# First half of batch 5 as seven block products, right sums of three batches placed anew

## The chip, the cores and the metric

The kernel runs on one core of a Trainium2 chip. The metric is the device time of one execution in microseconds (us); the time of a version is the median of its runs.

## What is computed

For each of 8 batches the input `x[b]` (1024 tokens, 512 features, float32) goes through two residual layers. Both are linear in `x` once the condition vector of the batch is known:

```python
# layer 0: a low-rank matrix per batch, from a small network on the condition
layer = base_layer[None] + einsum('bdr,bkr->bdk', x_a, x_b)      # rank 8
x = x + (x + einsum('btc,bco->bto', x, layer))
# layer 1: scaled weight
d = rsqrt(einsum('bi,io->bo', ys * ys, weight * weight) + 1e-8)  # ys = cond / sqrt(512)
x = x + (x + einsum('bsi,io->bso', x * ys[:, None, :], weight) * d[:, None, :])
```

So the output of a batch is `x[b]` times one 512 x 512 matrix of that batch, and the kernel builds these eight matrices (`q[b]`) first.

## The kernel before, in words

**Number format.** Float32 accuracy is made from two parts of each operand: a rounded high part and the rest (`h` and `l`, `ph` and `pl`, the two halves of `xs`). A product of two such operands takes three matmuls: high by high, high by rest, rest by high. ScalarE makes the high part by a cast, VectorE the rest by a subtraction that needs that cast.

**Plain tiles.** `main(b, t)` (L893) multiplies 128 tokens by `q[b]`: four chunks of 128 features, three matmuls each, so 12 matmuls of 512 columns into one bank `po`. ScalarE copies the bank to `o` and issues the store on its own queue. Tiles are numbered i = 8 b + t; `place(i)` names the spot behind tile i. The text calls "tile 36" the one with i = 36 (batch 4, t = 4). `split_x(b, j)` (L723) makes the operand `xs(b, j)` for two tiles, from a half batch `x(b, h)` that `load_x` (L719) brings in on SyncE's queue (1 MB).

**Seven products.** The last batches go by `Seven` (L905): a half batch g of 512 tokens is cut into 2 x 2 blocks, as `q[b]` is, and seven block products take the place of eight. A product is 12 matmuls of 256 columns. `make_sums` (L920) makes the right-hand sums of a batch: four subtractions `traw` of 512 columns on VectorE, two casts `th` of 1024 on ScalarE, two subtractions `tl` of 1024 on VectorE. `make_right` (L941) makes `ph` and `pl` of the batch. `make_left(g)` (L957) makes the left operands of a half: casts `xa`, `x22` and two `sh` on ScalarE; four sums `sraw`, then `xa`, `x22` and two `sl` on VectorE. It is a generator with six stops, and `part(g, steps)` (L1005) runs the seven products in the order 1, 5, 6, 2, 7, 3, 4, going one stop further in `steps` behind each. Products 1, 6, 7 and 4 add up in the same bank, `w`, which is emptied after each of them: by a ScalarE copy after 1, 6 and 4 and by a VectorE addition after 7. The next of them cannot start before that. Each part stores its 512 tokens on SyncE's queue.

**Buffers.** `x(b, h)`, `xs`, `xa`, the matrices `q[b]` and the `tl` tile of batch 5 share one pool, "big", of 8 buffers; `late_pools` (L1049) closes the pools of the earlier stages and opens those of the last.

**Order.** Matmuls keep the order of the program. The operations on VectorE, ScalarE and SyncE that go through `ve`, `se` and `sy` do so where `InOrder.on` is set, which is the case from behind the last tile on. While the tiles are emitted it is off (but for a few steps), and the planner of the programming layer puts each engine's instructions in the order of its list, by its own estimate of when they can run; it also decides which buffer of a pool a tile gets. On the chip each engine works its list from the top.

Before the change, batches 0 to 4 and the first half of batch 5 are plain tiles (0 to 43), and five parts follow: (5,1), (6,0), (6,1), (7,0), (7,1). The loop ends with:

```python
    InOrder.on = True
    load_x(NB - 2, 1)
    s5.part(1, s6.make_left(0))
```

Of the kernel before, what the change touches and what calls it, by code (L numbers as in the profile page):

```python
# [15 lines left out]
NB = 8  # L16
# [14 lines left out]
def cond_resid_kernel(ctx: ExitStack, tc: tile.TileContext, small, cond, condrows, consts,  # L31
# [47 lines left out]
    def big_tile(name, dtype=F32):  # L79
        return big.tile([P, KC, D], dtype, tag="big", name=name)  # L80
# [88 lines left out]
    def newton_rsqrt(v, sd, shape, name):  # L169

        r = sp.tile(shape, F32, name=f"r_{name}")
        ve.reciprocal(r, sd)
        t = sp.tile(shape, F32, name=f"t_{name}")
        ve.tensor_mul(t, r, r)
        ve.tensor_mul(t, t, v)
        ve.tensor_scalar(t, t, -0.5, 1.5, ALU.mult, ALU.add)
        return r, t
# [29 lines left out]
    r, t = newton_rsqrt(ve_l, sd, [NB, 1], "l")  # L207
# [86 lines left out]
    r, t = newton_rsqrt(v, sv, [P, KC, NB], "d")  # L294
# [163 lines left out]
    def rank_t():  # L458


        xb = with_bias(1)
        by = tmp_tile("by")
        ve.scalar_tensor_tensor(by, crow, SCALE, xb, ALU.mult, ALU.mult)
        hi, s = work_tile(), work_tile()
        se.copy(hi, by)
        yield
        ve.scalar_tensor_tensor(s, hi.bitcast(F32), neg_u, by, ALU.mult, ALU.add)
        by = s.bitcast(F32)
        yield
        pb = misc.tile([P, KC, P], F32, tag="misc", name="pb")  # L470
        for k in range(KC):
            turn(pb[:, k, :], by[:, k * P:(k + 1) * P], ident)
        byT = work_tile().rearrange("p (k c) -> p k c", k=KC)
        se.copy(byT, pb)
        yield
        pt = misc.tile([P, D], F32, tag="misc", name="pt_t")
        for k in range(KC):
            for i, w in enumerate((wh, wl)):
                mm(pt, byT[:, k, :], w[:, k, :], start=(k == 0 and i == 0),
                   stop=(k == KC - 1 and i == 1))  # L480
        t = tmp_tile("t")
        ve.tensor_mul(t, pt, drow)
        ve.scalar_tensor_tensor(t, xb, upper, t, ALU.mult, ALU.add)
        th, tl = work_tile(), work_tile()
        se.copy(th, t)
        yield
        ve.tensor_sub(tl, t, th.bitcast(F32))
        yield
        done = stack((th, tl), neg_t, "t", 0)
        yield  # L490
        stt[0] = done()
        yield
        late_rows.append(stack((th, tl), neg_t, "t", 1, rows[:, 3, :]))
        yield
# [208 lines left out]
    def p_tiles(b):  # L703
        ph[b] = ppool.tile([P, KC, D], F32R, tag="ph", name=f"ph_{b}")
        pl[b] = ppool.tile([P, KC, D], F32R, tag="pl", name=f"pl_{b}")
# [13 lines left out]
    def load_x(b, h):  # L719
        raw[b, h] = big_tile(f"x_{b}_{h}")  # L720
        sy.dma_start(raw[b, h], x[b, h])

    def split_x(b, j, part=None):  # L723

        t = raw[b, j // 2][:, :, (j % 2) * 2 * P:(j % 2 + 1) * 2 * P]
        if part != 1:
            xs[b, j] = big.tile([P, 2, KC, 2 * P], F32R, tag="big", name=f"xs_{b}_{j}")
            se.copy(xs[b, j][:, 0], t)
        if part != 0:
            hi, lo = xs[b, j][:, 0], xs[b, j][:, 1]  # L730
            ve.tensor_sub(lo, t, hi.bitcast(F32))
# [71 lines left out]
    steps = rank_t()  # L803
# [89 lines left out]
    def main(b, t):  # L893
        s = xs[b, t // 2]
        at = slice((t % 2) * P, (t % 2 + 1) * P)
        ps = po.tile([P, D], F32, tag="po", name=f"po_{b}_{t}")
        for c in range(KC):
            for i, (u, m) in enumerate(((0, ph[b]), (0, pl[b]), (1, ph[b]))):
                mm(ps, s[:, u, c, at], m[:, c, :],
                   start=(c == 0 and i == 0), stop=(c == KC - 1 and i == 2))  # L900
        o = pools["o"].tile([P, D], F32, tag="o", name=f"o_{b}_{t}")
        se.copy(o, ps)
        nc.scalar.dma_start(out[b, t * P:(t + 1) * P, :], o)
# [150 lines left out]
    NTT = NT // P  # L1054
    after = {}

    def at(b, t, f, *args):
        after.setdefault((b, t), []).append((f, args))
# [5 lines left out]
    place = lambda i: divmod(i, NTT)  # L1064
# [9 lines left out]
    for b, spots in ((4, [11 + n for n in spread]), (6, [21 + n for n in spread])):  # L1074
# [3 lines left out]
        for n, p in enumerate(Pair.ORDER):  # L1078
            spot = spots[2 * n]
# [5 lines left out]
        at(*place(first + 4), load_rank, b + 1)  # L1085
        at(*place(end), rank_term, b)
        at(*place(end + 1), rank_term, b + 1)
    for b, spot in ((4, 27), (5, 33)):
        for j in range(2):
            at(*place(spot + j), split_p, b, j)  # L1090

    s5, s6, s7 = (Seven(NB - i) for i in (3, 2, 1))

# [2 lines left out]
            pass  # L1096

    at(*place(31), late_pools)
    at(*place(34), s5.make_sums)
    at(*place(34), s5.share_right)  # L1100
    at(*place(35), s6.make_sums)
    at(*place(37), s7.make_sums)
    at(*place(38), load_x, NB - 3, 1)
    at(*place(39), all_left, s5, 1)
    at(*place(41), s6.make_right)
    at(*place(42), load_x, NB - 2, 0)

    TILES = (NB - 2) * NTT - NTT // 2
    for i in range(TILES):
        b, t = divmod(i, NTT)  # L1110
        if t == 0 and b + 1 < NB - 2:
            p_tiles(b + 1)
        main(b, t)
        if t % 4 == 0 and 0 < i < TILES - 4:
            load_x(*divmod(i // 4 + 1, NHALF))
        if t % 2 == 0 and i + 4 < TILES:
            split_x(*divmod(i // 2 + 2, NTT // 2))
        for f, args in after.get((b, t), ()):
            f(*args)
    InOrder.on = True  # L1120
    load_x(NB - 2, 1)
    s5.part(1, s6.make_left(0))
    load_x(NB - 1, 0)
    s6.part(0, s6.make_left(1))
    load_x(NB - 1, 1)
# [72 lines left out]
```

## Time and profile before

| what | us |
|---|---|
| median of 3 runs | 294.06 (293.91 to 294.32) |
| the profiled execution, its own time | 293.74 |
| its span, first to last instruction | 291.9 |
| TensorE busy | 286.3 (98%) |
| VectorE busy | 214.8 (74%) |
| ScalarE busy | 175.0 (60%) |
| mean granted clock of TensorE | 0.998 |

The page lists, for each engine, the busy time and its share of the span, then the chain of work that ended last, followed back from the end. In the timelines a row is: start, duration, engine, line, operation, what is written `<-` what is read, and in brackets the idle time before it with what ended it. PE is TensorE, PEld its weight loads, DVE VectorE, ACT ScalarE, SP SyncE. Durations of neighbouring rows can overlap by a tenth of a microsecond or more, since an engine starts the next instruction before the last one's result has landed.

### The profile page before, as it was taken

The page shows a single profiled execution, that of the slowest core. Times are in us where ns is not written, and L with a number is a line of the kernel's source. Part 1 is how long each engine was busy: PE and PEld are TensorE (multiplying, and loading weights), DVE is VectorE, ACT ScalarE, POOL GpSimd, SP SyncE. Part 2 cuts the span into 40 slices and gives each one's busy share as a digit, 9 for nine tenths or more (in the row PEclk, how much of TensorE's full clock was granted, in tenths as well). Part 3 has the DMA queues.
Part 4 walks back from the last instruction along what each step waited for, and adds up shares of the span by engine and source line. Part 5 has one row for each costly group of instructions (what it writes and reads, how often), then busy time and mean ns, then how long its engine had stood idle before and what let it go on. Part 6 is the DMA issues. An engine that isn't in the chain of part 4 may idle for free.

```text
span 291.9 us, 4100 instructions
## 1 busy us (share of the span) xinstructions
PE 286.3 (98%) x1519; PEld 225.2 (77%) x1519; DVE 214.8 (74%) x295; ACT 175.0 (60%) x272; POOL 35.9 (12%) x77
## 2 busy tenths in 40 slices
PE   7999999999999999999999999999999999999995
PEld 3665566467877878888877888887888889999994
DVE  2889898989916999519799565326789977798912
ACT  5757263286849884658654575544658745856641
POOL 2111000202944560000022000000000000000000
PEclk9999999999999999999999999999999999999999
DMA  7999999992799783332328114262175870852334
GB/s 209 405 429 413 411 403 405 390 383 90 187 321 322 235 250 116 110 145 93 159 80 263 55 72 135 83 216 74 72 251 176 291 257 1 290 204 87 142 146 144
DMA packets 19924, 62.14 MB, mean 213 GB/s; under 512 B 2736, under 2 KB 4016, under 8 KB 15552
## 3 DMA queue, kind: packets, MB, share of 16 engines
q1 hardware_dynamic: 9504, 43.76, 40.7%
q10 hardware_dynamic: 6912, 12.32, 11.5%
q0 software_dynamic: 3488, 5.79, 7.5%
q8 instruction: 12, 0.20, 0.3%
q14 instruction: 8, 0.07, 0.1%
HBM read 44.02 MB, written 17.84 MB: 212 GB/s over the span
## 4 chain that ended last, share of the span: by engine, by line
PE 96%; DMA 2%; ACT 0%; DVE 0%; SPq 0%; ACTq 0%; issue 0%
PE po L45 42%; PE pp L45 20%; PE sw L45 9%; PE px L45 5%; PE sz L45 5%; PE pg L45 4%; PE pq L45 4%; PE sv L45 2%; DMA b_raw<-in_baseT 2%; PE pr L45 1%; PE pt_t L45 1%; PE ps_t L45 0%; PE pq_v L45 0%; PE pq_z L45 0%; ACT o L62 0%; DVE o L62 0%
## 5 line engine op out<-in xcount | busy, mean ns | idle before, releaser
L45 PE MATMUL po<-ph,xs 128*128 128x512 f32 x352 | 113.7, 392 | 0.0
L45 PEld LDWEIGHTS po<-ph,xs 128*128 128x128 f32 x352 | 66.0, 188 | 15.6 <-issue 1.7
L45 PE MATMUL po<-pl,xs 128*128 128x512 f32 x176 | 68.6, 390 | 0.0
L62 ACT COPY o<-po 128x512 f32<-128x512 f32 x44 | 25.9, 588 | 35.0 <-PE po L45 35.0
L45 PEld LDWEIGHTS po<-pl,xs 128*128 128x128 f32 x176 | 33.0, 188 | 6.7
L62 DVE TENSOR_TENSOR xs<-x,xs 128x1024 fp32r<-128x1024 f32 (+1 forms) x23 | 27.0, 1176 | 15.0 <-ACT xs L62 15.0
L62 DVE TENSOR_TENSOR nl_p<-n,nh_p 128x1024 fp32r<-128x1024 f32 x21 | 25.7, 1222 | 12.4 <-ACT nh_p L62 12.4
L62 ACT CAST nh_p<-n 128x1024 fp32r<-128x1024 f32 x21 | 22.1, 1054 | 14.6 <-DVE n L62 10.9
L62 ACT CAST xs<-x 128x1024 fp32r<-128x1024 f32 x22 | 23.0, 1056 | 3.6 <-DMA x<-in_x 3.6
L62 ACT COPY q<-pp 128x512 f32<-128x512 f32 x30 | 17.4, 586 | 8.7 <-PE pp L45 8.6
L542 POOL DMA_DIRECT2D fa<-kept_a x28 | 13.8, 508 | 58.3 <-PE pr L45 54.0
L45 PE MATMUL pp<-nh_p,sh 128*128 128x512 f32 x48 | 19.0, 396 | 0.0
L45 PE MATMUL pp<-nh_p,sl 128*128 128x512 f32 x48 | 18.7, 390 | 0.0
L45 PE MATMUL pp<-nl_p,sh 128*128 128x512 f32 x48 | 18.7, 390 | 0.0
L62 DVE SCALAR_TENSOR_TENSOR n<-w_sb,ysT,d 128x512 f32<-128x512 f32 x24 | 16.9, 748 | 0.9 <-DMA d<-d_out 0.9
L62 ACT CAST sh<-sraw 128x1024 fp32r<-128x1024 f32 (+1 forms) x14 | 12.9, 926 | 6.8 <-DVE sraw L62 6.8
L62 DVE TENSOR_TENSOR sl<-sraw,sh 128x1024 fp32r<-128x1024 f32 (+1 forms) x14 | 14.9, 1067 | 2.2 <-ACT sh L62 2.2
L62 DVE TENSOR_TENSOR pl<-q,ph 128x1024 fp32r<-128x1024 f32 (+1 forms) x10 | 11.1, 1116 | 6.9 <-ACT ph L62 6.9
L45 PE MATMUL px<-w,hT 128*32 128x512 f32 x128 | 15.6, 599 | 0.0
L62 ACT COPY o<-sw 128x512 f32<-128x512 f32 (+1 forms) x12 | 6.2, 518 | 15.4 <-PE sw L45 12.3
L62 DVE TENSOR_TENSOR q<-pr,q 128x512 f32<-128x512 f32 x14 | 8.8, 688 | 7.9 <-PE pr L45 7.8
L62 DVE TENSOR_TENSOR n<-n,n 128x1024 f32<-128x1024 f32 x12 | 14.5, 1225 | 0.1
(199 smaller groups left out, 576.6 us busy)
## 6 DMA issues: line engine op xcount, KB each, us to landing
w<-in_w SPq DMA_DIRECT2D x16, 1024.0 KB, 10.4
x<-in_x SPq DMA_DIRECT2D x16, 1024.0 KB, 5.6
out<-o ACTq DMA_DIRECT2D x44, 256.0 KB, 2.3
out<-o SPq DMA_DIRECT2D x8, 512.0 KB, 2.9
fa<-kept_a POOLq DMA_DIRECT2D x28, 64.0 KB, 2.7
ft<-kept_t POOLq DMA_DIRECT2D x28, 64.0 KB, 3.5
d<-d_out POOLq DMA_DIRECT2D x6, 256.0 KB, 7.3
w_sb<-in_w SPq DMA_DIRECT2D x1, 1024.0 KB, 8.5
```

The lines of the kernel that those rows point to most:

```text
L45: tc.keep_in_program_order(nc.tensor.matmul(*args, **kw))
L62: return lambda *a, **kw: pin(f(*a, **kw)) if InOrder.on else f(*a, **kw)
L542: nc.gpsimd.dma_start(fold[name, b][32 * c:32 * c + 32, :], kept[name, g][32 * i:32 * i + 32, :])
```

## The change

The first half of batch 5 becomes a part (5,0) of seven products, ahead of (5,1), so that plain tiles end with tile 39. `split_p` and `split_x` for batch 5 fall away; `make_right` of batch 5 and `all_left` of (5,0) come in behind tiles 33 and 34. The right sums of batches 5, 6 and 7 stand behind tiles 31, 36 and 38, where they stood behind 34, 35 and 37. The left operands of (5,1), made at once behind tile 39 before, are now made step by step during part (5,0), one product later than in the other parts; `make_right` of batch 6 moves from behind tile 41 into part (5,1). All sums are VectorE subtractions and additions, as before.

```diff
-    for b, spot in ((4, 27), (5, 33)):
-        for j in range(2):
-            at(*place(spot + j), split_p, b, j)
+    for j in range(2):
+        at(*place(27 + j), split_p, 4, j)
...
     at(*place(31), late_pools)
-    at(*place(34), s5.make_sums)
-    at(*place(34), s5.share_right)
-    at(*place(35), s6.make_sums)
-    at(*place(37), s7.make_sums)
-    at(*place(38), load_x, NB - 3, 1)
-    at(*place(39), all_left, s5, 1)
-    at(*place(41), s6.make_right)
-    at(*place(42), load_x, NB - 2, 0)
-
-    TILES = (NB - 2) * NTT - NTT // 2
+    at(*place(31), s5.make_sums)
+    at(*place(32), load_x, NB - 3, 0)
+    at(*place(33), s5.make_right)
+    at(*place(34), all_left, s5, 0)
+    at(*place(36), load_x, NB - 3, 1)
+    at(*place(36), s6.make_sums)
+    at(*place(38), s7.make_sums)
+
+    def one_later(steps):
+        yield
+        yield from steps
+
+    TILES = (NB - 3) * NTT
     for i in range(TILES):
         b, t = divmod(i, NTT)
-        if t == 0 and b + 1 < NB - 2:
+        if t == 0 and b + 1 < NB - 3:
             p_tiles(b + 1)
         main(b, t)
...
     InOrder.on = True
+    load_x(NB - 2, 0)
+    s5.part(0, one_later(s5.make_left(1)))
     load_x(NB - 2, 1)
-    s5.part(1, s6.make_left(0))
+    s5.part(1, s6.make_left(0), then=s6.make_right)
     load_x(NB - 1, 0)
```

## The prediction

> **What bounds the kernel now.** I read the page's totals and chain first, then the table by stretches from 205 us on, then the timelines of TensorE (PE), ScalarE (ACT), VectorE (DVE) and SyncE (SP) around the places that the change touches, and last the order in which the two built programs list their instructions on each engine. That order decides this case.
>
> ```profile
> PE 286.3 (98%) x1519; PEld 225.2 (77%) x1519; DVE 214.8 (74%) x295; ACT 175.0 (60%) x272; POOL 35.9 (12%) x77
> PE 96%; DMA 2%; ACT 0%; DVE 0%; SPq 0%; ACTq 0%; issue 0%
> ```
>
> The chain that ends last is TensorE for 96% of the span, so any product that is saved shows in the time, and so does any moment in which TensorE waits. But the share of VectorE hides how unevenly it is loaded. By stretches (from:to, length, then busy us of PE, PEld, DVE, ACT, POOL):
>
> ```profile
> 212.00:217.00 5.00, 5.00 (x24) 4.14 (x23) 4.45 (x7) 3.07 (x4) 0.00 (x0) 1.00 0.82 302
> 227.00:238.00 11.00, 11.00 (x51) 9.13 (x50) 10.93 (x15) 7.08 (x10) 0.00 (x0) 1.00 0.88 302
> 238.00:248.00 10.00, 10.00 (x85) 10.00 (x85) 6.12 (x8) 5.99 (x9) 0.00 (x0) 1.00 0.11 42
> ```
>
> Just before the seven-product part starts (238 us), VectorE is busy for 10.93 of 11 us, without TensorE waiting once. There is no reserve there, and that is where the change adds work.
>
> **What the change saves.** In the chain (start, length), tiles of batch 4 and 5 and then the first products:
>
> ```profile
> 202.40 35.59 PE po L45 x156
> 237.98 1.43 PE sw L45 x12
> 239.42 1.44 PE sz L45 x12
> ```
>
> 156 matmuls are 13 tiles (31 to 43): 2.72 us a tile. A product is 1.44 us. Four tiles of batch 5 (10.88 us) become seven products (10.08 us), and the built list does hold all 84 matmuls of them: 0.80 us saved, 0.27% of 294.06. More than that it cannot bring.
>
> **What it moves: the first hold-up, at tile 36.** The sums of batch 5 now take a buffer of the pool "big" behind tile 31 rather than 34. The load of x(4,1) therefore gets another buffer; the built program makes it wait for the last matmul of tile 29 (198.5 us) where it waited for a subtraction that ended at 191.7. It still lands by about 204 (5.4 us from issue to landing). But the planner's list now has the cast of xs(4,2) on ScalarE behind the copy of tile 35, where it stood ahead of the copy of tile 30. Tile 36 multiplies with that cast. What stands there in the trace (ACT, PE; start, duration):
>
> ```profile
> 216.26 0.59 ACT L62 COPY o<-po 128x512 f32<-128x512 f32 x1 [1.50 <-PE po L45]
> ...
> 220.07 1.05 ACT L62 CAST xs<-x 128x1024 fp32r<-128x1024 f32 x1
> ...
> 221.70 0.59 ACT L62 COPY o<-po 128x512 f32<-128x512 f32 x1 [0.58 <-PE po L45]
> 222.18 1.05 ACT L62 CAST xs<-x 128x1024 fp32r<-128x1024 f32 x1
> ```
> ```profile
> 215.83 0.62 PE L45 MATMUL po<-ph,xs 128*128 128x512 f32 x2
> 216.29 0.39 PE L45 MATMUL po<-pl,xs 128*128 128x512 f32 x1
> 216.51 0.62 PE L45 MATMUL po<-ph,xs 128*128 128x512 f32 x2
> ```
>
> The first copy is that of tile 35. The last two rows of ACT show that its list is kept in order: it idles 0.58 us for tile 37, though the cast behind the copy has had its data (load issued at 210.81) since about 216. So in the changed kernel: copy 216.26, cast from 216.74 (0.48 later) to 217.79, VectorE's rest 217.82 to 219.05. The low half is needed by the third matmul of tile 36, at 216.51 before and at about 219.1 after: **2.6 us late**. Tiles 37 to 39 follow at 2.72 us; tile 39 ends at 229.5. Waiting behind that cast are also xs(4,3) (needed at 224.1 by tile 38, ready by 220.2, free) and, on VectorE, everything that follows.
>
> **The second hold-up: VectorE's list up to the last product.** Steps on VectorE start 1.14 us apart (1024 columns) or 0.60 us (512), results come at 1.23 and 0.69:
>
> ```profile
> 215.76 1.29 DVE L62 TENSOR_TENSOR traw<-q 128x512 f32<-128x512 f32 x2
> 216.97 1.41 DVE L62 TENSOR_TENSOR traw<-q,traw 128x512 f32<-128x512 f32 x2
> 218.77 2.36 DVE L62 TENSOR_TENSOR tl<-traw,th 128x1024 fp32r<-128x1024 f32 x2 [0.39 <-ACT th L62]
> ```
>
> The new list behind tl of batch 5 (done by 214.7) is: xs(4,2), xs(4,3), left operands of (5,0), the sums of batch 6, the sums of batch 7, four sraw steps and xa of (5,1), and only then the addition that empties product 7 of (5,0). VectorE idles from 214.7 to 217.8 for the late cast. Then:
>
> - xs twice, to 220.1; three sraw, to 221.9; wait for ACT's xa, which stands behind the copy of tile 36 (222.05 + 1.05), to 223.1;
> - xa 1.14, sraw 0.60, x22 0.60, sl twice 2.4: to 227.9;
> - batch 6: four traw 2.6, to 230.5; wait for th, whose casts stand behind the copy of tile 39 (230.2 + 1.05), to 231.3; tl twice 2.4: to 233.7;
> - batch 7: four traw 2.6, to 236.3; wait for th, to 236.7; tl twice 2.4: to 239.1;
> - (5,1): four sraw 2.5, xa 1.14: to 242.7; the addition, to 243.4.
>
> TensorE meanwhile: products 1 and 5 from 229.5 to 232.4; product 6 waits 0.35 us, since the copy of product 1's bank stands on ACT behind the two th casts of batch 6 (done 232.7); 6, 2, 7, 3 to 238.5. Product 4 adds onto the bank of product 7, so it waits for the addition: 238.5 to 243.5, **5.0 us**. Part (5,1) starts at 244.9 instead of 237.8. Before, the sums of batches 6 and 7 (9.8 us of VectorE) ran from 215.76 to 228.2, beside tiles and ahead of any product; their cover was tiles 36 to 43, of which four are gone, and the left operands of (5,0) stand ahead of them now (6.5 us: four sraw 2.5, xa 1.1, x22 0.6, sl 2.3), against 2.3 us of removed xs steps.
>
> **Is it won back later?** No: from there on TensorE needs 10.08 us a part, VectorE 7.8 us (the 6.5, and two additions at 0.6) and 1.7 more in two of them (pl); both catch up with each other and TensorE is bound again. The walk leaves the nearest step, pl of batch 6, about 0.2 us ahead of its use. Edits that I cost at nothing: SP loses no time with two stores more (512 KB, 2.9 us to land); x(6,1) now queues behind them, issued about 245 and landed about 251 (5.4 us), first read at 257; four stores fewer on ACT's queue; POOL does nothing in this stage; steps "one product later" move xa of (5,1) on ACT only, which is early (234).
>
> **Sum**, against the profiled execution (293.74 us, span 291.9, so 1.84 outside): -0.80 + 2.6 + 0.35 + 5.0 = +7.15. How soon TensorE multiplies after a wait is not in the trace of this stage; from nothing to one weight load, 0.19 us (its LDWEIGHTS rows), at two waits, it makes +7.15 to +7.5. I take +7.2, since weights are loaded beside other work: 300.9 for such an execution, and the median, 0.32 above it, goes from 294.06 to **301.3**.
>
> **What a standing TensorE costs besides.** Nearest row: the first matmuls after standing still.
>
> ```profile
> 0.99 4.04 PE L45 MATMUL warm<-zero 128*128 128x512 bf16 x11 [0.99 <-DVE eps_l L62]
> ```
>
> 11 in 4.04 us is 0.367 each against 0.227 for 512 columns later: 1.54 us lost. Bounds for the two long waits: nothing, or 1.54 each, 3.1 together. I take nothing for the likeliest, since 1.07 us of standing still at 5.03 was soon followed by normal spacing (four in 1.10 us from 7.21), and keep 3.1 for the range. The Trainium skill (TensorE: Matmul & The Clock Gate, "Part 1: The HAM clock gate") says that the clock halves after one idle window of about 3.4 us, windows running freely. By it the 2.1 us gap would pass and the 5.0 us one hold a whole window about every other time; with 1.7 us lost the sum would be 303.0, an estimate from that page.
>
> **Rivals.**
> - The clock drops after the waits: +1.5 to +3.1 more, 302.8 to 304.4. For it the warm row, against it the gap at 5.03. Chance 0.32.
> - Only tile 36 and product 6 are late: VectorE keeps pace, if its steps ran some 20% faster or the additions of (5,0) overtook. +2.6 + 0.35 - 0.8 = 296.2. Against it, the list and the 10.93 of 11. Chance 0.07.
> - Faster: ACT's cast of xs(4,2) is done before 216.0, and VectorE reaches product 7's addition by 235.5: then only -0.80, 293.3. It decides from a cast 1.8 us earlier than the list lets it be. Chance 0.03.
> - Forecast, 300.6 to 301.9: 0.56. Beyond 304.4 or between the cases: 0.02.
>
> About 0.2% (0.6 us) is what a measurement of this kernel tells from no change. Range: 300.3 (forecast less VectorE's uncertainty of 4% on 25 us) to 304.4 (both clock costs). Slower 0.96, same 0.01, faster 0.03.
>
> **What would show it.** Right: no tile matmul between about 216.1 and 217.8; PE waiting 5 us for DVE's o<-sw in the seventh product of (5,0); DVE with gaps of no more than 2 us together from 223 to 247; part (5,1) starting near 245; a clock of 1.00 behind the wait. Wrong: a cast of xs ahead of tile 35's copy, the addition of product 7 within 2 us of that product, or a span under 298.

## The result, and the profile after

The changed kernel takes 303.43 us (median of 4 runs, 302.89 to 305.11) against 294.0 us of the kernel before on the same chip: 1.033 times as long, 95% interval 1.031 to 1.035. The profiled execution took 302.89 us with a span of 301.1, so it is 9.15 us longer than the profiled one of before (293.74). The page's totals and its chain:

```profile
PE 289.0 (96%) x1555; PEld 227.8 (76%) x1555; DVE 219.7 (73%) x303; ACT 176.3 (59%) x275; POOL 36.1 (12%) x77
PE 91%; DVE 4%; ACT 2%; DMA 2%; issue 0%; ACTq 0%; SPq 0%
```

TensorE carries 91% of the chain instead of 96%, and VectorE and ScalarE, which had none of it, now hold 6% together. Where that is, the table of TensorE's waits says (total us, times, longest):

```profile
PE sw L45 <- DVE o L62: 4.7, 1, 4.7
PE po L45 <- ACT xs L62: 2.1, 1, 2.1
...
PE po L45 <- DVE xs L62: 0.5, 1, 0.5
...
PE sw L45 <- ACT sv L62: 0.2, 1, 0.2
```

These are the places that the prediction had named: product 4 of (5,0), tile 36 twice (its first matmul, then its third), and product 6. The timeline of ScalarE at tile 36 (start, duration), and below it that of TensorE:

```profile
216.40 0.59 ACT L62 COPY o<-po 128x512 f32<-128x512 f32 x1 [2.13 <-PE po L45]
217.02 0.34 ACTq L903 DMA_DIRECT2D out<-o  x1
217.40 1.99 ACT L62 CAST xs<-x 128x1024 fp32r<-128x1024 f32 x2 [0.41 <-ACT o L62]
```
```profile
215.98 0.39 PE L45 MATMUL po<-ph,xs 128*128 128x512 f32 x1
218.50 0.50 PE L45 MATMUL po<-ph,xs 128*128 128x512 f32 x1 [2.13 <-ACT xs L62]
...
219.76 0.73 PE L45 MATMUL po<-ph,xs 128*128 128x512 f32 x2 [0.53 <-DVE xs L62]
...
233.09 0.28 PE L45 MATMUL sz<-th,sl 128*128 128x256 f32 x1
233.56 0.39 PE L45 MATMUL sw<-th,sh 128*128 128x256 f32 x1 [0.19 <-ACT sv L62]
...
239.30 0.28 PE L45 MATMUL sz<-ph,sl 128*128 128x256 f32 x1
244.32 0.39 PE L45 MATMUL sw<-th,x 128*128 128x256 f32 x1 [4.75 <-DVE o L62]
```

The cast of xs(4,2) does stand behind the copy of tile 35, and begins 0.66 us later than the walk had it (217.40 for 216.74): 0.14 us because the copy itself is that much later in this execution, the rest because the issue of that tile's store lies between the two. The last row is product 4; the row at 233.56 is product 6. On VectorE the addition that it waits for comes straight behind the work for (5,1):

```profile
242.45 1.22 DVE L62 TENSOR_TENSOR xa<-x,xa 128x1024 fp32r<-128x1024 f32 x1
243.58 0.69 DVE L62 TENSOR_TENSOR o<-sw,o 128x512 f32<-128x512 f32 x1
```

What was not in the sum is seen by stretches (from:to, length, busy us of PE, PEld, DVE, ACT, POOL, then the granted clock):

```profile
244.50:246.00 1.50, 1.50 (x9) 1.50 (x10) 1.50 (x3) 0.00 (x0) 0.00 (x0) 0.59 0.00 0
246.00:248.00 2.00, 2.00 (x12) 2.00 (x11) 1.97 (x4) 0.59 (x1) 0.00 (x0) 0.50 0.46 175
248.00:250.00 2.00, 2.00 (x18) 2.00 (x18) 1.97 (x4) 1.01 (x2) 0.00 (x0) 0.95 1.01 348
```

Behind the wait TensorE works at half its clock. A clock of 0.50 leaves 0.59 and 0.95 as means only if it fell at 244.8 and came back at 248.2: 3.4 us. The chain shows the price; of its 24-matmul steps, the first stands behind the wait, the second behind none:

```profile
244.32 4.63 PE sw L45 x24
256.15 2.88 PE sw L45 x24
```

A part of the difference comes with any wait: at full clock a step of this length behind one takes 3.13 us (the kernel with both gaps filled, below). So the clock costs about 1.5 us there. The four runs have mean clocks of 0.994, 0.989, 0.989 and 0.981, in the order of their times (302.89, 303.35, 303.5, 305.11). Twice what a mean lacks of 1, times the span, is the time at half clock: 3.6, 6.6, 6.6 and 11.5 us. The profiled run is the one with the least of it.

### The profile page after: what moved, and what is told of

Its sections match the earlier page's. It is cut to its first block, busy times and chain, and to the rows that moved or that the text cites. A ratio compares the mean times of both kernels' runs of the same rounds, so it can differ in the third digit from the quotient of the medians.

```text
span 301.1 us, 4181 instructions
## 1 busy us (share of the span) xinstructions
PE 289.0 (96%) x1555; PEld 227.8 (76%) x1555; DVE 219.7 (73%) x303; ACT 176.3 (59%) x275; POOL 36.1 (12%) x77
## 4 chain that ended last, share of the span: by engine, by line
PE 91%; DVE 4%; ACT 2%; DMA 2%; issue 0%; ACTq 0%; SPq 0%
PE po L45 37%; PE pp L45 19%; PE sw L45 10%; PE px L45 5%; PE sz L45 5%; PE pg L45 4%; PE pq L45 4%; PE sv L45 2%; DMA b_raw<-in_baseT 2%; DVE tl L62 2%; PE pr L45 1%; DVE sraw L62 1%; ACT th L62 1%; ACT o L62 1%; DVE traw L62 1%; PE pt_t L45 1%
## 5 line engine op out<-in xcount | busy, mean ns | idle before, releaser
L45 PE MATMUL po<-ph,xs 128*128 128x512 f32 x320 | 104.3, 393 | 2.7 <-ACT xs L62 2.1
L45 PEld LDWEIGHTS po<-ph,xs 128*128 128x128 f32 x320 | 60.0, 188 | 17.8 <-ACT xs L62 2.6
L45 PE MATMUL po<-pl,xs 128*128 128x512 f32 x160 | 62.4, 390 | 0.0
L62 ACT COPY o<-po 128x512 f32<-128x512 f32 x40 | 23.6, 589 | 41.2 <-PE po L45 41.2
L62 DVE TENSOR_TENSOR xs<-x,xs 128x1024 fp32r<-128x1024 f32 (+1 forms) x21 | 24.4, 1171 | 16.9 <-ACT xs L62 16.9
L45 PEld LDWEIGHTS po<-pl,xs 128*128 128x128 f32 x160 | 30.0, 188 | 6.1
L62 ACT CAST xs<-x 128x1024 fp32r<-128x1024 f32 x20 | 20.8, 1054 | 2.9 <-DMA x<-in_x 2.5
L62 ACT CAST sh<-sraw 128x1024 fp32r<-128x1024 f32 (+1 forms) x16 | 15.0, 943 | 8.7 <-DVE sraw L62 8.7
L62 DVE TENSOR_TENSOR sl<-sraw,sh 128x1024 fp32r<-128x1024 f32 (+1 forms) x16 | 17.2, 1085 | 1.4 <-ACT sh L62 1.4
L45 PE MATMUL sw<-th,x 128*128 128x256 f32 x48 | 10.6, 302 | 4.7 <-DVE o L62 4.7
```

Source lines behind the costliest of these rows:

```text
L45: tc.keep_in_program_order(nc.tensor.matmul(*args, **kw))
L62: return lambda *a, **kw: pin(f(*a, **kw)) if InOrder.on else f(*a, **kw)
```

## The experiments

**The sums of batch 5 later.** Edit:

```diff
-    at(*place(31), s5.make_sums)
+    at(*place(33), s5.make_sums)
```

> The changed kernel with the right sums of batch 5 behind tile 33 instead of 31, nothing else. Theory (two hold-ups, both from the order of the lists): x(4,1) gets its earlier buffer again, the cast of xs(4,2) stands ahead of tile 30's copy, tile 36 is on time (3.1 us back), VectorE reaches the addition of product 7 some 6 us earlier; left are about 1.4 us before product 7 (its bank's copy stands behind the th casts of batch 7) and 0.5 us before product 4, and no drop of the clock: 294.0 - 0.8 + 1.9 = 295.1 (294.7 to 295.7). Rival 1 (the sums of batches 6 and 7 alone set the date of product 4, the late cast only shows ahead of it): product 4 starts as late as before, 301 to 303. Rival 2 (the clock drops after any wait of TensorE): 296.7.

Measured 297.84 us (297.10 to 298.00), ratio 1.012 (1.010 to 1.014). Tile 36 no longer waits, so the place of the early sums is the cause of the first hold-up. The load of x(4,1) is issued at 191.95 again, as before the change (191.78), and not at 198.71 as with it, which fits the buffer that they take. But waits of 2.2, 1.1 and 0.3 us are left in (5,0), and the time is some 2.7 us above what I had expected. The timeline of VectorE and the list of DMA issues (KB, us to landing) of this kernel show a new cause:

```profile
212.21 1.29 DVE L62 TENSOR_TENSOR traw<-q 128x512 f32<-128x512 f32 x2 [3.26 <-DMA out<-o]
```
```profile
x<-in_x SPq DMA_DIRECT2D x1, 1024.0 KB, 5.4
...
out<-o ACTq DMA_DIRECT2D x1, 256.0 KB, 5.5
```

The first subtraction of batch 5 waits 3.3 us for a store. The row names no tile; by the buffers it is the store of tile 31, and a kernel below tries it. That store is issued at 206.17, just behind the load of x(5,0) at 205.54, and lands after 5.5 us; in the changed kernel, where the load starts at 210.96, it lands after 2.0. The clock has a share too: it is 1.00 in the profiled run (297.10), and 0.992 to 0.994 in the other three, which take 0.7 to 0.9 us longer.

**Matmuls nobody needs in the gap before product 4.** Edit: in `part`, ahead of product 4 of (5,0):

```diff
+                if p == 4 and (self.b, g) == (NB - 3, 0):
+                    fill = po.tile([P, D], F32, tag="po", name="fill")
+                    (lh, _), _ = self.left[g][1], self.right[1]
+                    for _ in range(16):
+                        mm(fill, lh[:, 0, 0:P], ph[self.b][:, 2, :], start=True, stop=True)
```

> The changed kernel with 16 matmuls of 512 columns (3.6 us, into a bank that nobody reads) between products 3 and 4 of part (5,0), so that TensorE stands still for about 1.1 us there instead of 4.75. Theory (the half clock behind the wait comes of standing still): product 4 starts at the same time, the clock stays at 1.00, 303.4 - 1.6 = 301.8 (301.4 to 302.2). Rival (the drop has another cause, such as the load of VectorE or the DMAs at that moment): clock 0.5 behind the wait as before, 303.4 or more.

Measured 302.87 us (302.61 to 303.18): neither number. Product 4 waits only 1.1 us now, and the clock stays at 1.00 behind it. In its profile the clock fell at the other gap, after tile 36, where it had held in the profile of the changed kernel:

```profile
219.00:220.00 1.00, 0.47 (x2) 0.30 (x2) 1.00 (x2) 0.34 (x1) 0.00 (x0) 0.98 0.00 0
220.00:222.00 2.00, 2.00 (x6) 1.51 (x5) 2.00 (x4) 0.00 (x0) 0.00 (x0) 0.50 0.27 33
222.00:224.00 2.00, 2.00 (x8) 1.59 (x7) 0.58 (x1) 0.12 (x1) 0.00 (x0) 0.66 0.71 295
```

The step of 46 matmuls from tile 36 on takes 12.36 us in this chain and 10.76 in that of the changed kernel: 1.6 us, much the same price at another place. So one long pause is covered and the other still takes its price.

**Without the sums of batch 7.** Edit (batch 7's products read batch 6's sums):

```diff
-    at(*place(38), s7.make_sums)
+    at(*place(38), lambda: s7.right.update({p: s6.right[p] for p in (5, 6, 7, 4)}))
```

> The changed kernel without the right sums of batch 7 (left out: 4.9 us of VectorE and two casts; the products of batch 7 read the sums of batch 6 in their place). Theory: tile 36 is as late as in the changed kernel (3.1 us) and product 6 by 0.2, but the addition of product 7 is reached in time, TensorE does not wait for product 4 and its clock does not drop: 303.4 - 4.75 - 1.6 = 297.1 (296.5 to 297.4). Rival (the addition is late for another reason, the late tiles or the left operands of (5,1) alone): TensorE still waits several us before product 4, 300 or more.

Measured 297.69 us (297.61 to 299.21), ratio 1.012 (1.010 to 1.015): a little above the theory's range, and far from the rival's 300. With 4.7 us less of work for VectorE (215.0 for 219.7 busy) product 4 does not wait at all; the 2.1 and 0.5 us at tile 36 are as before. The clock fell behind tile 36 in this profile too (0.78 on average from 216 to 222).

**Both.** The edits of the first and the third kernel together.

> Both at once: the right sums of batch 5 behind tile 33, and the right sums of batch 7 left out (the products of batch 7 read those of batch 6). Theory: no hold-up is left and only the saving of the seven products shows: 294.0 - 0.8 = 293.2 (293.0 to 293.5). Rival (the part (5,0) is not cheaper than four tiles in place, or another wait comes up): 294.0 or more.

Measured 294.12 us (293.74 to 294.65), ratio 1.000 (0.9985 to 1.0009). Both long waits are gone and the clock is 0.998 or more in every run. The expected gain of 0.8 us is taken back by one wait of 1.0 us, of product 6 for ScalarE's copy of product 1's bank; this kernel's sums wait for the store of tile 31 as in the first one (3.19 us).

**Both gaps filled.** Edit: as in the second kernel, and in `main`, in front of tile 36:

```diff
+        if (b, t) == (4, 4):
+            for _ in range(9):
+                mm(ps, xs[4, 1][:, 0, 0, 0:P], ph[4][:, 0, :], start=True, stop=True)
```

> The changed kernel with matmuls that nobody needs laid into both long waits: nine of 512 columns (9 x 0.227 = 2.04 us, of a gap of 2.13) in front of the first matmul of tile 36, written into that tile's own bank before its first real product starts it anew, and sixteen (3.63 us, of a gap of 4.75) before product 4 of (5,0). No data gets faster, so tile 36 and product 4 start when they did. Theory (a long pause makes the clock fall to half, whichever pause it is; one fall costs 1.6 us): no pause longer than about 1.1 us is left, the granted clock is 1.00 in every stretch and every run, and the time is that of the profiled run after less one fall, 302.89 - 1.6 = 301.3 us, range 301.0 to 301.8, with little spread between runs. Rival (the clock falls for another reason, such as the burst of products of 256 columns after tile 43): the clock stays at 0.99 and the time at 302.6 to 303.6.

Measured 301.34 us (301.25 to 301.35), with clocks of 0.999 or 1.00 in all four runs. The timeline of TensorE shows the nine in place of the pause, and the stretches show a clock that never falls:

```profile
215.88 3.02 PE L45 MATMUL po<-ph,xs 128*128 128x512 f32 x11
```
```profile
216.00:222.00 6.00, 5.38 (x23) 3.83 (x22) 3.61 (x5) 2.58 (x3) 0.00 (x0) 1.00 0.35 110
...
244.00:248.00 4.00, 3.77 (x31) 3.78 (x32) 3.97 (x6) 1.19 (x3) 0.00 (x0) 1.00 0.26 95
```

Its step behind the wait of product 4, in the chain:

```profile
244.22 3.13 PE sw L45 x24
```

Useful work was as late as before (third matmul of tile 36 at 219.67 for 219.76, product 4 at 244.22 for 244.32); only the pauses were filled. That took 2.1 us off the median and nearly all of the spread. Of the 9.4 us of the change, 7.3 are waits less the saving, and 2.1 are the clock. This is a gain by work that does nothing, and no version to keep.

**The late pools one tile earlier.** Edit, on the first kernel:

```diff
-    at(*place(31), late_pools)
+    at(*place(30), late_pools)
```

> The kernel of the right sums of batch 5 behind tile 33 once more, with the late pools opened behind tile 30 instead of 31. In that run the first subtraction of these sums waited 3.3 us for the store of tile 31, because its buffer lies where that tile's o lay, and that store took 5.5 us instead of 2.0 beside the 1 MB load of x(5,0), which now starts at 205.5. With the pools opened one tile earlier, the sums wait for the store of tile 30 (issued about 203.4, landed about 205.5) instead. Theory (this store is where the 2.7 us went that I had not expected in the first run): sums done by about 212 as in the changed kernel, no wait of product 4; product 6 still waits 1.1 to 1.4 us for ScalarE's copy of product 1's bank; -0.8 + 1.1 to 1.4 = +0.3 to +0.6: 294.5 us, range 294.0 to 295.2, clock 1.00. Rival (VectorE's list is too long for this place anyway): 296.5 to 298, as with the pools behind tile 31.

Measured 294.40 us (median of 13; 12 of them 294.27 to 294.78), ratio 1.0013 (1.0004 to 1.0022). So the wait for the store was where the first kernel lost 3.4 us, the clock's share behind its waits included. The profiled execution of the new kernel, its slowest, runs 3.2 us late from a load near 80 us on (the copy of tile 28 at 197.76, for 194.60 in the changed kernel), so its rows are to be read that much earlier:

```profile
208.55 1.29 DVE L62 TENSOR_TENSOR traw<-q 128x512 f32<-128x512 f32 x2 [0.33 <-issue]
...
239.31 0.69 DVE L62 TENSOR_TENSOR o<-sw,o 128x512 f32<-128x512 f32 x1
```

The addition of product 7 starts at about 236.1 by the changed kernel's time, 7.4 us earlier than there, though all sums of batches 6 and 7 stand ahead of it. TensorE's only wait in this stage is 1.4 us at product 6.

**The sums of batch 7 in part (6,0).** Edit, on the kernel before this one: `make_sums` of batch 7 becomes a generator; its subtractions are listed ahead of (6,0), its casts and low parts behind that part's first product; left operands of (5,1) not delayed, those of (6,1) two products later, `make_right` of batch 6 in (5,0).

> A version that should win: right sums of batch 5 behind tile 33, late pools behind tile 30, and the right sums of batch 7 not behind tile 38 but step by step in part (6,0), where VectorE has idle time before they are needed in (7,0); the left operands of (5,1) are not one product later, and those of (6,1) start two products later; pl of batch 6 is made in part (5,0). All work is done. Theory (what the seven products save is 0.80 us, and it shows once VectorE is even): two short waits of TensorE are left, 0.2 and 0.4 us in batch 6, so 294.0 - 0.8 + 0.2 to 0.6: 293.6 us, range 293.2 to 294.0, clock 1.00. Rival (batch 7's sums only move the wait into batch 6): a wait of 1 us or more in (6,0) or (6,1) and 294.4 us or more.

Measured 293.84 us (293.50 to 294.65, 12 runs), ratio 0.9991 (0.9979 to 1.0002): inside the expected range, yet not told apart from the kernel before. Up to part (5,1) nothing waits, so the chain of this kernel shows the saving by itself:

```profile
202.56 24.75 PE po L45 x108
227.31 1.43 PE sw L45 x12
...
235.94 2.88 PE sw L45 x24
```

The last row is product 4 of (5,0) and product 1 of (5,1), which so starts near 237.38, 34.82 us behind tile 31. Before the change these were 35.58 us (202.40 to 237.98): 0.76 us are saved. They are lost again in (6,0) and (6,1), where VectorE is the tight engine now. The stretches show 0.10 and 0.17 us in which TensorE stands still:

```profile
250.00:262.00 12.00, 11.90 (x99) 11.70 (x99) 11.86 (x15) 9.57 (x14) 0.00 (x0) 1.00 0.60 198
262.00:275.00 13.00, 12.83 (x107) 12.63 (x106) 12.93 (x17) 10.16 (x15) 0.00 (x0) 1.00 0.40 155
```

A wait costs more than this idle time, because a matmul's row (0.28 us) reaches beyond the start of the next (0.12 us later without a wait). By their starts the two products come 0.26 and 0.33 us late, and their second matmuls another 0.1 us each: nearly 0.8 us together.

**The left operands not one product later.** Edit, on the changed kernel:

```diff
-    s5.part(0, one_later(s5.make_left(1)))
+    s5.part(0, s5.make_left(1))
```

> The changed kernel with one part undone: the steps for the left operands of (5,1) start with the first product of (5,0), as for the other batches, instead of one product later. Theory (the order in which VectorE's list is written decides): a further step, the low part of the left sums, comes before the addition that empties product 7, and ScalarE's copy too stands behind the casts of these sums, so TensorE waits longer at (5,0), some 6.5 us in place of 4.75: 303.4 + 1.5 = 304.9 us, range 304.2 to 306.0. Rival, as the prediction had it (the delay moves only work of ScalarE that is early anyway): 303.0 to 303.8.

Measured 306.29 us (305.60 to 306.87), beyond the range expected. The wait moves from product 4 to product 7 (table of waits), and two products more are behind it:

```profile
PE sw L45 <- ACT o L62: 6.2, 1, 6.2
```
```profile
244.36 2.93 PE sw L45 x12
247.28 2.56 PE sz L45 x12
249.84 3.07 PE sw L45 x24
```

Product 7 waits for ScalarE's copy of product 6, which stands behind the cast of a left sum of (5,1); that sum is on VectorE behind the sums of batch 7. TensorE resumes at 244.36, as in the changed kernel (244.32), but with 24 matmuls (2.88 us) more to do. Not all of this is the order of the lists, for the clock fell at both gaps in this profile (0.79 from 216 to 222, 0.50 from 244 to 250). Behind tile 36, where it held in the profile of the changed kernel, the fall made what follows 1.4 us later (the copy of tile 39 at 231.96 for 230.54). Without it the lists alone would cost about 1.5 us, an estimate from these rows that agrees with the theory. At the second gap the clock fell inside the wait and came back at 250.2, after 6.8 us. The three steps above take 8.56 us, where 6.0 would do at full clock.

**The store of tile 35 on SP.** Edit:

```diff
-        nc.scalar.dma_start(out[b, t * P:(t + 1) * P, :], o)
+        queue = nc.sync if (b, t) == (NB - 4, 3) else nc.scalar
+        queue.dma_start(out[b, t * P:(t + 1) * P, :], o)
```

> The changed kernel with the store of tile 35 issued by SP instead of ScalarE; nothing else. In the changed kernel this store stands on ScalarE's list between the copy of tile 35 and the cast of xs(4,2), and the cast began 0.41 us after the copy had ended. Theory (the store's issue holds up the cast): the cast starts within 0.1 us of the end of the copy, or overlaps it as casts behind copies do elsewhere, TensorE's wait for it in front of tile 36 falls from 2.13 to between 1.6 and 1.75 us; the time is 0 to 0.5 us less, since the rest is taken by product 4's wait, and depends on how often the clock falls. Rival (the cast waits for something else, such as its input): the wait stays at 2.1 us.

One run, 303.45 us. The cast follows the copy at once, and tile 36 starts half a microsecond earlier (timelines of ScalarE and TensorE):

```profile
216.42 0.59 ACT L62 COPY o<-po 128x512 f32<-128x512 f32 x1 [2.13 <-PE po L45]
216.90 1.99 ACT L62 CAST xs<-x 128x1024 fp32r<-128x1024 f32 x2
```
```profile
218.00 0.50 PE L45 MATMUL po<-ph,xs 128*128 128x512 f32 x1 [1.62 <-ACT xs L62]
```

So the store's issue was what held the cast up. In the time it brings nothing: on SP's list the load of x(5,0) now stands behind that store and is issued at 217.51 instead of 210.96, VectorE waits for it until 222.74, product 6 waits 0.9 us instead of 0.2, and product 4 still 4.8. The clock held behind tile 36 and fell inside the wait for product 4, from 241.9 to 248.8 by the stretches:

```profile
238.00:242.00 4.00, 1.75 (x15) 1.55 (x13) 3.93 (x5) 1.08 (x2) 0.00 (x0) 0.99 0.00 0
242.00:244.00 2.00, 0.00 (x0) 0.00 (x0) 2.00 (x4) 2.00 (x3) 0.00 (x0) 0.50 0.00 0
248.00:250.00 2.00, 2.00 (x16) 2.00 (x16) 1.97 (x4) 0.51 (x2) 0.00 (x0) 0.80 0.78 295
```

The 24-matmul step behind the wait takes 5.01 us here, 1.9 more than the 3.13 at full clock.

## Why the prediction was right, and where it was not

The forecast was 301.3 us as the likeliest time, and the rival "the clock drops after the waits" was put at 302.8 to 304.4. The median, 303.43, lies with that rival, and outside the 300.6 to 301.9 of the forecast itself. The waits were walked right but for half a microsecond, and the term that failed is the clock, which the sum took at nothing.

- **Saved, 0.80 us:** 0.76, by the chain of the kernel with the sums of batch 7 in (6,0). No kernel here kept it to the end: that one lost it again to two short waits, and its median is not told apart from that of before.
- **Tile 36, taken as 2.6.** The third matmul came at 219.76 instead of 216.6 (where it would have followed tile 35 without a wait): 3.1. The mechanism is shown by the first kernel (the wait vanishes with the sums moved), the missed 0.5 by the last one (the store's issue on ScalarE's list). The walk went from the copy straight to the cast, and counted stores on ScalarE's queue only as four fewer, at no cost.
- **Product 6, taken as 0.35:** 0.35, counted as the walk counts, from start to start (233.56, for 233.21 at 0.12 us behind the matmul before). The 0.2 of the table is the idle time.
- **Product 4, taken as 5.0:** 4.9, counted so (244.32 for 239.42). That VectorE's list decides is shown by the kernel without the sums of batch 7. But the reason given, that there was no reserve for the added work, is only half of it. With the sums at tile 33 and the pools opened at tile 30 VectorE does the same work and the addition is in time. What the changed kernel lacked was the time that VectorE stood still for late data, which the walk has as steps but not as the reason: 3.58 us for the cast of xs(4,2), 1.30 for xa, 1.04 and 0.81 for casts of th. One late cast thus cost twice, at tile 36 and at product 4.
- **The sum of the waits,** -0.8 + 3.1 + 0.35 + 4.9 = 7.55, stands beside the 7.2 of the prediction; the store's issue is the difference. The kernel with both gaps filled measures it: 7.6 us between the profiled executions (301.33 and 293.74), 7.3 between the medians (301.34 and 294.0). That its median meets the 301.3 of the forecast so closely is luck in part: the forecast was 300.9 for a profiled execution, plus 0.32 up to the median, and this kernel showed no such distance.
- **The clock, taken as 0 of up to 1.54 for each wait.** This is the step that failed. A fall of 3.4 us cost 1.5 to 1.6 us, so the warm row had the right size for it. But where the clock fell inside the wait, it stayed down for 6.8 and 6.9 us, and cost 2.6 and 1.9 (the last two kernels). The longest run, 305.11 us, lies beyond the 304.4 that the prediction gave for both waits. The row set against it, a pause of 1.07 us at 5.03, was too short to speak for pauses of 3 and 5 us.
- **Taken as nothing, and not nothing:** the delay of the left operands. The prediction had it move "on ACT only"; its removal costs 2.9 us by the medians, about 1.5 of them because the left sums put ScalarE's casts in front of the copy of product 6, the rest by the clock. The rest of that list (two stores more on SP, the later load of x(6,1), four stores fewer on ScalarE's queue) was not tried by itself.

The Trainium skill (TensorE: Matmul & The Clock Gate, "Part 1: The HAM clock gate") speaks of windows of about 3.4 us that run freely, and of half the clock after an idle one. The stretches agree in length: from 244.8 to 248.2 here, and, worked out in the same way, 220.0 to 223.4 in the kernel with sixteen matmuls filled in; the 6.8 and 6.9 us are about twice as long. They agree that the same gap need not cost the same in each run. They do not agree with the reading that the prediction made of it, that tile 36's gap would pass: between the last matmul of tile 35 and the third of tile 36 lie 3.4 us with two matmuls in them, and in three of the five profiles that have this gap the clock fell behind it. So a window need not be empty. The 3.4 us ahead of a fall hold 0.48 us of TensorE's busy time at product 4 here, 0.78 to 0.99 at tile 36 in those three, and 1.25 in the kernel with the store on SP. If windows of 3.4 us are laid end to end backwards from the falls, an estimate from that page's length, those that held a part of a gap and kept the full clock have 1.57 us or more.

Left open is whether in the 305.11 us run both gaps took their price; its 11.5 us at half clock would fit it, but it has no profile. The rule by which a window counts as idle is open too: no run varied the work inside a gap in small steps.

## What to carry to other kernels

A buffer taken one tile earlier moves a load, the load moves a cast, and the cast's place in an in-order list decides; walk each list to the last instruction, the issue of stores included, and let every stall of one engine delay the lists of the others. Where a walk ends with pauses of TensorE of 2 us or more and little work around them, add at least one fall of the clock, here 1.5 to 1.6 us, to the likeliest value and not to the range alone, and leave room above for a longer one. When a mend falls short, look at what its earlier load now runs beside: here the store that the next step waited for.

## What the runs showed of the hardware that was not expected

- A store of 256 KB landed after 5.5 us instead of 2.0 when a 1 MB load had been issued 0.6 us before it.
- The issue of one store (0.34 us on ScalarE's queue) between a copy and a cast held the cast up: TensorE's wait behind it was 2.13 us with it and 1.62 without.
- The clock halved for 3.4 us, or for 6.8 to 6.9 us where it fell inside the pause. It did so even around a gap of 3.4 us that held two matmuls (0.73 us busy), and at which gap it did so changed from profile to profile.
- Waits whose rows show 0.17 and 0.19 us of idle time made TensorE's next matmul 0.33 and 0.35 us late.
